# Writing down the order: the scheduler's order against the written one in the first layer's attention

## The chip, the cores and the metric

The kernel runs on one core of a Trainium2 chip. The core has TensorE (PE in the profile, its weight loads PEld), VectorE (DVE), ScalarE (ACT), GpSimd (POOL) and SyncE (SP), which here only issues DMAs. Each engine takes its instructions from a queue of its own, in order; they wait for each other by semaphores. The time is device microseconds of one execution, here the median of three runs.

## The reference

Four sequences of 512 tokens of width 128 go through two layers, all in f32. The first layer is a half-step of a "latent" block, a full attention and another half-step of the same latent block; the second layer mixes chosen tokens, runs four additive-attention blocks and mixes chosen tokens again.

```python
x = x + 0.5 * _L0_ffn_ref(_layernorm(x), ...)    # latent: causal attention, then mixture of experts
x = x + _L0_attn_ref(_layernorm(x), ...)         # full attention, 16 heads of 8
x = x + 0.5 * _L0_ffn_ref(_layernorm(x), ...)
x = x + 0.5 * _L1_ffn_ref(...)                   # chosen tokens
x = x + _L1_attn_ref(...)                        # four blocks
x = x + 0.5 * _L1_ffn_ref(...)
```

The change concerns the first three lines. `_L0_ffn_ref` normalizes x, runs a causal attention with 16 heads of 8, normalizes again, and sends each token to the best two of eight experts (hidden width 256, SiLU).

## The kernel before, in words

**Tasks and units.** `first_layer` makes twelve tasks: four causal ("latent") ones, one for each sequence, four full ones, four causal ones. They are numbered 0 to 11. A task is cut into units, each of which covers one 128x512 PSUM bank of scores for each of four row groups: 10 units in a causal task, 16 in a full one, 144 in all. Heads lie four to a row group; g counts the column groups of four heads.

**The loop.** `attention` walks once over all units, n = 0 to 151, and each step has two halves ("half-units"). In a step, three units are at work: unit n has its scores computed and their maxima taken (`maxima`, L527, PE; `reduce_max`, L543 for causal and L547 for full tasks, DVE); a unit five or six before has its scores computed again, transposed and with the maximum subtracted (`shifted`, L562, PE), then the exponential (`exponent`, L574, ACT) and, in causal tasks, the mask on the diagonal (`mask`, L580, POOL); a unit two steps before that is multiplied by the values (`products`, L605, PE).

When the last unit of a group g has its maxima, `place_maxima` transposes them (`mT`, L551, DVE) and four DMAs on SP (L555) write them into rows of `qA`, where L562 reads them as one more row of the contraction.

**What runs beside the units.** A half-unit also holds pieces of other work, written as generators that are stepped once per half-unit. `prepare` (L298 on) makes the next task's input during the present one: bn_stats of two chunks of X (L167); a half-unit later the other two and the aggregates `mv` (L171), then on POOL `v` (L312, in causal tasks also L316) and the root `r` (L154); a half-unit later four `h` (L323, POOL; task 0's on DVE); a half-unit later four `Y` (L336, POOL; in full tasks L328), then the transposes of `h` (L193, PE) and their copy (ACT). The projections (L267), their copies `qC` and `kC` and the DMAs that spread them over `qA` and `kA` (L363 to L366, SP) follow. A task's `prepare` begins with the first units of the task before it.

`gates` follows a causal task: the same kind of normalization with `h` in L686 on POOL, the gate's scores, a copy `lg` (L703), comparisons `more` and `same` on DVE (L709, L711) with two operations on POOL (L712, L718), `rank` (L725), `ex` (L727, ACT), `comb` (L731 to L737), and transposes of `comb` (L741, PE). Then `Mixture` adds, per half-unit, one expert half: L267 on PE, `th` (L467, ACT), `v` (L472, DVE), `hid` (L473, POOL), and three half-units later L267 again into `sum`.

**Banks.** `bank` picks one of eight PSUM banks by a small clock kept while the kernel is written out; the choice is made when the text is run and is the same whatever order the instructions get later.

**What sets the order.** The kernel's text is written out once as a list of instructions. A scheduler of the framework then puts each engine's instructions into an order of its own: it respects what they read and write and the buffers of the pools, and may otherwise move an instruction ahead of others that stand before it in the text. Two aids keep instructions where they are written: `tc.issue_after`, which is used once for the constants, and `tc.keep_in_program_order` for DMAs that load late weights. Here, `prepare`'s lines that the following speaks of:

```python
yield from moments_steps(X[:, b], mv)
...
r = rsqrt(v[:, 0:n], n)
yield
eng = nc.gpsimd if self.k else nc.vector
...
yield
```

Of the kernel before, what the change touches and what calls it, by code (L numbers as in the profile page):

```python
# [40 lines left out]
def tile_macaron(ctx: ExitStack, tc: tile.TileContext, a: dict, out: bass.AP):  # L41
    nc = tc.nc
# [68 lines left out]
    def constants_later():  # L111
        nc.gpsimd.tensor_copy(ident_h, ident)

        make_causal_mask(nc, paired, mask_val=NEG)
        nc.gpsimd.memset(paired[KSEL:P, 0:KSEL], NEG)

        nc.gpsimd.affine_select(
            out=before,
            in_=ones[:, 0 : NE * NE].rearrange("p (e f) -> p e f", f=NE),
            pattern=[[1, NE], [-1, NE]],  # L120
            compare_op=ALU.is_gt,
            fill=0.0,
            base=0,
            channel_multiplier=0,
        )

        nc.gpsimd.iota(
            slots, pattern=[[1, KSEL]], base=1, channel_multiplier=0, allow_small_or_imprecise_dtypes=True
        )
        nc.gpsimd.iota(  # L130
            places, pattern=[[1, T]], base=0, channel_multiplier=0, allow_small_or_imprecise_dtypes=True
        )

        nc.gpsimd.memset(mine, 0.0)
        for r in range(NPAIR):
            for i in range(2):
                nc.gpsimd.memset(mine[i * KSEL : (i + 1) * KSEL, r, 2 * r + i : 2 * r + i + 1], 1.0)

    def in_turn(runs):

        t = 0
        while runs:
            for start, run in list(runs):
                if start <= t and next(run, 0) == 0:
                    runs.remove((start, run))
            t += 1
# [85 lines left out]
    def first_layer(opened, picked):  # L232
        with (
# [18 lines left out]
            def heads_constants():  # L252
                constants()
                for i, vA in enumerate(vAs):

                    nc.gpsimd.memset(vA, 0.0)
                    split = vA.rearrange("p c (u s) k -> p (c u) s k", s=2)
                    for i in range(2):
                        nc.gpsimd.memset(split[:, :, i, 16 * i + HD : 16 * i + 2 * HD], 1.0)
                constants_later()  # L260
# [501 lines left out]
                heads_constants()  # L762
            tasks[0].spread()
            tasks[0].values()
            attention()
            streaming.close()
            top = opened()
            choosing = choice([0, 1], lambda b: (1, b) in mixed, top, picked)
# [524 lines left out]
    with ExitStack() as until_chosen:  # L1293

        def opened():
            return until_chosen.enter_context(tc.tile_pool(name="top", bufs=1, side="right"))

        chosen_first = first_layer(opened, {})
        made = tc.tile_pool(name="made", bufs=2)
        wp, ready = until_done.enter_context(made), {}  # L1300
        weights = additive_weights(wp, ready)
        chosen_attention(*chosen_first, beside=[(8, weights(0))])
# [73 lines left out]
```

## Time and profile before

| what | value |
|---|---|
| median of three runs | 1370.44 us (1369.15 to 1373.41) |
| span of the profiled execution | 1369.7 us |
| instructions in the profile | 29349 |
| PE busy | 1289.1 us (94%) |
| DVE busy | 954.4 us (70%) |
| ACT busy | 586.5 us (43%) |
| POOL busy | 562.1 us (41%) |
| mean granted TensorE clock | 0.968 |

For the profiled execution the profile gives its span and no other time; the span is 0.7 us below the median. The first layer's units take the span up to about 815 us. Times in the text are microseconds from the span's start. A line of the profile names the engine, the source line, the operation and the tiles, out<-in; "x4" counts merged instructions; what stands in brackets is the idle time of the engine before it and what ended it. A line of the list of waits has the engine and its instruction, who released it, then the total in us, how often, and the longest. A line of the table by stretches has, after the stretch and its length, the busy time and count of PE, PEld, DVE, ACT and POOL, the granted clock, the DMA share and GB/s. "PEld" idle times are not stalls where PE itself is busy.

### The profile page before, as it was taken

How to read it: one execution, taken by the hardware profiler on the slowest of the kernel's cores; microseconds unless marked ns; L12 is line 12 of the kernel's file. 1: busy time of each engine (PE TensorE's matmuls, PEld its weight loads, DVE VectorE, ACT ScalarE, POOL GpSimd, SP SyncE). 2: the span in 40 equal slices, each digit the busy share in tenths (PEclk: the TensorE clock that was granted, in tenths of full speed). 3: DMA queues.
4: the chain of work that ended last, by engine and by line, in shares of the span. 5: the costliest groups of instructions: out<-in, count | busy, mean ns of one | idle time of the engine just before them, and what ended most of it. 6: DMA issues, size and time to landing. Idle time of an engine off the chain costs nothing. (4 is left out here: it accounts for less than half of the span.)

```text
span 1369.7 us, 29349 instructions
## 1 busy us (share of the span) xinstructions
PE 1289.1 (94%) x11050; PEld 699.9 (51%) x11050; DVE 954.4 (70%) x3293; ACT 586.5 (43%) x1180; POOL 562.1 (41%) x823
## 2 busy tenths in 40 slices
PE   5998999999999999999999999989889999997897
PEld 2554445333333333465544443367667767665675
DVE  6886776666658777778767638687466776667773
ACT  1555454454556666665545443222223332323222
POOL 8345655544424112024564755622244443543100
PEclk8999999999999999999999999999979999999799
DMA  3001101020111100000111011211000100000000
GB/s 115 21 24 41 43 33 49 2 80 1 64 45 32 39 1 18 3 19 19 50 33 34 33 53 28 76 40 40 1 20 5 40 1 17 1 1 1 1 9 23
DMA packets 37172, 39.52 MB, mean 29 GB/s; under 512 B 11080, under 2 KB 23880, under 8 KB 37032
## 3 DMA queue, kind: packets, MB, share of 16 engines
q1 hardware_dynamic: 34536, 35.06, 8.3%
q10 hardware_dynamic: 2496, 2.59, 0.6%
q8 instruction: 87, 1.43, 0.4%
q14 instruction: 53, 0.43, 0.1%
HBM read 29.45 MB, written 1.18 MB: 22 GB/s over the span
## 5 line engine op out<-in xcount | busy, mean ns | idle before, releaser
L574 ACT ACTIVATE e<-bank 128x512 f32<-128x512 f32 x576 | 313.7, 595 | 278.4 <-PE bank L527 240.0
L527 PE MATMUL bank<-kA,qA 32*128 32x512 f32 (+3 forms) x1536 | 349.0, 527 | 4.1 <-DVE nm L543 1.8
L562 PE MATMUL bank<-qA,kA 32*128 32x512 f32 (+3 forms) x1536 | 334.0, 524 | 0.3 <-DVE nm L543 0.3
L543 DVE CUSTOM_DVE_ANT_0 junk<-bank,causal 128x384 f32<-128x384 f32 (+3 forms) x512 | 251.0, 490 | 89.5 <-PE bank L527 51.3
L547 DVE TENSOR_REDUCE nm<-bank 128x1 f32<-128x512 f32 x256 | 164.9, 686 | 78.9 <-PE bank L527 78.7
L473 POOL TENSOR_TENSOR hid<-v,spread 128x512 f32<-128x512 f32 x128 | 163.9, 1286 | 127.1 <-DVE v L472 101.7
L562 PEld LDWEIGHTS bank<-qA,kA 32*128 32x128 f32 x1536 | 129.5, 185 | 136.9 <-issue 54.1
L605 PE MATMUL sum<-e,vA 128*32 128x256 f32 (+1 forms) x2560 | 183.7, 368 | 6.1 <-POOL e L580 6.0
L580 POOL TENSOR_SCALAR_AFFINE_SELECT e<-e 128x256 f32<-128x256 f32 x256 | 99.3, 407 | 192.8 <-ACT e L574 191.7
L527 PEld LDWEIGHTS bank<-kA,qA 32*128 32x128 f32 x1536 | 147.4, 187 | 24.6 <-DVE nm L543 5.8
L605 PEld LDWEIGHTS sum<-e,vA 128*32 128x32 f32 x2560 | 62.8, 109 | 165.8 <-issue 134.0
L267 PE MATMUL sum<-hid,sb_f_w 128*32 128x512 f32 x1024 | 135.6, 597 | 3.0 <-POOL hid L473 2.9
L267 PE MATMUL bank<-tT,sb_f_w 128*32 128x512 f32 x1024 | 137.1, 602 | 0.0
L472 DVE SCALAR_TENSOR_TENSOR v<-th,bank 128x512 f32<-128x512 f32 x128 | 87.0, 681 | 43.9 <-ACT th L467 29.2
L467 ACT ACTIVATE th<-bank 128x512 f32<-128x512 f32 x128 | 76.3, 597 | 49.0 <-PE bank L267 39.5
L154 POOL TENSOR_TENSOR r<-v,mhalf 128x4 f32<-128x4 f32 (+1 forms) x64 | 71.8, 1123 | 5.1
L1250 PE MATMUL bank<-h2T,w 128*128 128x512 f32 x128 | 69.0, 632 | 0.2 <-ACT h2T L1239 0.2
L1256 PE MATMUL bank<-w,hid 128*128 128x128 f32 x512 | 65.7, 277 | 0.1
L1256 PEld LDWEIGHTS bank<-w,hid 128*128 128x128 f32 x512 | 63.1, 194 | 4.8 <-issue 1.5
L1251 ACT ACTIVATE hid<-bank,sb_l_cols 128x512 f32<-128x512 f32 x64 | 43.9, 688 | 39.9 <-PE bank L1250 39.8
L1148 PE MATMUL bank<-wa,hT 128*128 128x385 f32 x128 | 56.5, 540 | 1.4 <-ACT hT L1141 1.4
L312 POOL TENSOR_SCALAR v<-mv 128x4 f32<-128x4 f32 x12 | 2.8, 230 | 131.1 <-DVE mv L171 130.8
(279 smaller groups left out, 1805.4 us busy)
## 6 DMA issues: line engine op xcount, KB each, us to landing
spread<-away SPq DMA_DIRECT2D x64, 256.0 KB
qA<-mT SPq DMA_DIRECT2D x192, 2.0 KB
qA<-qC SPq DMA_DIRECT2D x11, 256.0 KB
kA<-kC SPq DMA_DIRECT2D x11, 256.0 KB
w<-in_l_w_dram SPq DMA_DIRECT2D x8, 256.0 KB
sb_m_wqkv<-in_m_wqkv_dram SPq DMA_DIRECT2D x4, 384.0 KB
m_yg<-in_m_trig_dram SPq DMA_DIRECT2D x8, 130.0 KB
X<-in_x_dram SPq DMA_DIRECT2D x4, 256.0 KB
```

What stands on the lines that cost most here:

```text
L267: nc.tensor.matmul(ps[32 * j : 32 * j + 32, :], lhsT=w[:, 32 * j : 32 * j + 32], rhs=rhs, start=start, stop=stop, skip_group_check=True,)
L467: nc.scalar.activation(th, ph, AF.Tanh, scale=0.5)
L472: nc.vector.scalar_tensor_tensor(v, th, 1.0, ph, ALU.add, ALU.mult)
L473: nc.gpsimd.tensor_tensor(hid, v, self.spread[e], op=ALU.mult)
L527: nc.tensor.matmul(ps[:, at : at + w], lhsT=t.qA[r0 : r0 + 32, g, c * P : (c + 1) * P], rhs=t.kA[r0 : r0 + 32, g, 0:w], start=True, stop=True,
L543: nc.vector.tensor_tensor_reduce(junk[:, 0:w], src, causal[:, T - w : T], 1.0, NEG, ALU.add, ALU.max, dst)
L547: nc.vector.tensor_reduce(dst, src, axis=AX.X, op=ALU.max)
L562: nc.tensor.matmul(ps[:, at : at + w], lhsT=t.kA[r0 : r0 + 32, g, kc * P : (kc + 1) * P], rhs=t.qA[r0 : r0 + 32, g, q0:T], start=True, sto ...
L574: nc.scalar.activation(es[n][:, j, :], ps, AF.Exp)
L580: nc.gpsimd.affine_select(out=e, in_=e, pattern=[[0, 2], [1, P]], compare_op=ALU.is_ge, fill=0.0, base=0, channel_multiplier=-1,)
L605: nc.tensor.matmul(to[32 * j : 32 * j + 32, q0 + lo - at : q0 + hi - at], lhsT=t.vA[:, kc, 4 * j + g, :], rhs=es[n][:, j, lo:hi], start=fresh,
L1256: nc.tensor.matmul(pm[:, c * P : (c + 1) * P], lhsT=hid[:, f, c * P : (c + 1) * P], rhs=w2[:, f, :], start=(f == 0), stop=(f == 3),)
```

## The change

After `attention()` has written its instructions, a new function `pinned` goes through those instructions and ties each one on DVE, POOL, PE and ACT to the one before it on the same engine, by a dependency without a semaphore. The scheduler thereby loses its choice on these four engines for the units' stretch; SP is not in the set. What comes before `attention()` (the first task's `prepare`, the constants) and behind it (the rest of the mixture, the second layer) is left to the scheduler as before.

```diff
+    def pinned(engines, since):
+
+        last = {}
+        for i in list(nc.cur_bb.bb.instructions)[since:]:
+            if i.engine in engines:
+                if i.engine in last:
+                    tc.add_manual_dep(
+                        i,
+                        last[i.engine],
+                        mybir.DependencyInfo(mybir.DependencyClass.NoSync, mybir.DependencyReason.DATA),
+                        reason="program order",
+                    )
+                last[i.engine] = i.name
+
     def in_turn(runs):
...
             tasks[0].spread()
             tasks[0].values()
+            since = len(nc.cur_bb.bb.instructions)
             attention()
+            pinned({mybir.EngineType.DVE, mybir.EngineType.Pool, mybir.EngineType.PE, mybir.EngineType.Activation}, since)
             streaming.close()
```

In the two built programs each engine has the same instructions. PE's order is the same. On DVE, 2621 instructions, task 2's last aggregate goes from place 32 to 104, that of task 8 from 634 to 742. On POOL, 823 instructions, task 2's first `h` goes from place 59 to 79. The transposes `mT` (L551) stand up to eight reductions later.

## The prediction

> **What bounds the kernel now.** I read the sums by stage first, then TensorE's waits, then the timeline around each stall. By stage (columns: stretch, its length, then busy us of PE, PEld, DVE, ACT, POOL with counts, granted clock, DMA share, GB/s):
>
> ```profile
> 21.00:64.00 43.00, 38.28 (x336) 20.76 (x336) 34.94 (x143) 17.62 (x33) 24.45 (x47) 0.88 0.06 18
> 90.00:116.00 26.00, 21.47 (x215) 11.75 (x216) 17.76 (x78) 11.71 (x23) 18.85 (x34) 0.87 0.01 2
> 250.00:270.00 20.00, 18.80 (x164) 8.49 (x162) 10.98 (x24) 7.96 (x15) 6.84 (x13) 0.83 0.01 2
> 400.00:557.00 157.00, 157.00 (x1444) 55.89 (x1440) 116.53 (x218) 97.88 (x183) 31.40 (x41) 1.00 0.08 23
> 640.00:665.00 25.00, 21.98 (x210) 12.62 (x209) 18.09 (x73) 11.85 (x23) 18.22 (x32) 0.93 0.01 1
> ```
>
> The attention of the first layer runs to about 815 us, and TensorE is busy in nearly all of it (157.00 of 157.00 us in the fourth row). What it waits for is therefore added to the end. The waits of PE up to 815 us (us in total, times, longest):
>
> ```profile
> PE sum L605 <- POOL e L580: 6.0, 2, 3.7
> PE bank L193 <- POOL h L323: 4.4, 4, 3.5
> ```
>
> The first is two stalls, at 106.7 and 648.2 us. The second is almost wholly one: task 1's transposes wait 3.45 us for `h` at 26.47 (three more waits of 0.30 follow it). At the transposes of tasks 2 to 11 PE waits 0.27 us at most. Why, task 8 shows: its `h` is made 80 us ahead (GpSimd, then PE):
>
> ```profile
> 420.52 1.67 POOL L154 TENSOR_TENSOR r<-v,mhalf 128x8 f32<-128x8 f32 x1
> 422.29 3.13 POOL L323 TENSOR_SCALAR h<-X,mv,r 128x128 f32<-128x128 f32 x4
> ...
> 505.16 0.66 PE L193 MATMUL bank<-ident,h 128*128 128x128 f32 x4
> ```
>
> **The change, part by part.** Instructions, shapes and counts stay. In the built program PE's order is the same in both kernels, ScalarE moves seven small `ex` (L727) and one copy, and SyncE's queue shifts by five places at most. What moves is VectorE and GpSimd, above all `prepare`: `mv` of task 2 goes from place 32 on VectorE to 104, of tasks 7 to 10 from 625, 634, 714, 795 to 661, 742, 825, 900. PE still reaches the transposes at its old place, so each task's chain must now fit in the two half-units that the text leaves it.
>
> *The chain of one `prepare`.* Behind the last reduction of its half-unit: two bn_stats and four bn_aggr 0.8 us (0.87 for four stats and 0.36 for the aggregates at 412.78); handover 0.1; `v` 0.57 for two (420-422 us: L312, L316, then `r`) or 0.3 for one; `r` 1.67 (128x8, causal tasks) or 1.04 (128x4, full tasks); handover 0.1; four `h` 3.13; the last transpose 0.3. That is 6.7 us causal, 5.8 full. Masks (0.4 each, L580) or `hid` (1.27, L473) that now stand between on GpSimd come on top. From the reduction's end in the profile to the transposes' end there were:
>
> - task 2: reduction 61.60, +6.7, two masks 0.8: 69.1 for 64.80, +4.3
> - task 3: 105.64, +6.7 +0.8: 113.1 for 115.55 (a time that holds the stall at 106.7): -2.4
> - task 4: 200.58, +5.8 +0.4 +1.3: 208.1 for 206.00, +2.1
> - task 5: 273.64, +5.8 +0.4: 279.8 for 278.12, +1.7
> - task 6: `hid` ends 361.57, +3.4: 365.0 for 364.01, +1.0
> - task 7: 441.65, +5.8: 447.4 for 444.99, +2.4
> - task 8: 502.48, +6.7: 509.2 for 505.82, +3.4
> - task 9: 564.00, +6.7: 570.7 for 566.66, +4.0
> - task 10: 604.35, +6.7 +0.4: 611.4 for 607.48, +3.9
> - task 11: behind a gate's `h` chain on GpSimd; 645.00 +0.8, `v` 0.9, `r` 1.5, two masks 0.8, `h` 2.4, then mask, `v`, `r`, mask, `h`, transpose 6.5: 658 for 655.53, +2.5
>
> Sum 22.9, I take **23**. Behind each stalled transpose stand on PE the next half-unit's scores, so VectorE and ScalarE starve too. Bounds 13 to 26: below, where VectorE is the pace (it has no idle time over 0.3 us from 36 to 64) it still holds about 2 us of scores and part of the stall is covered; above, the list with one more mask each.
>
> *The start.* Task 1's `mv` (done at 12.8 before) now stands behind two units of reductions, which end at 26.01. With 1.2 of stats, `v` 0.5, `r` 1.67, `h` begins at 29.7 for 25.62, so PE's 3.45 us wait grows by about 4. Unit 3 shifts by 4, and its eight reductions now stand ahead of the first `mT` (L551, 30.11 before): 39.5, its four DMAs until 41.7 and some 1.6 to land (packets of the last end at about 33.9 for an issue at 32.29). The first L562 starts at about 43.3 for 36.51. VectorE works on in that time, so it loses 5 and PE 7. I take **6**, bounds 4 and 9. The later 47 `mT` come 1 to 5 us later and keep 1 us or more between landing and the L562 that reads them (tightest at 85 and 458 us); they cost nothing, and about 1 us a task if that cover is gone (inside the upper bound). On SyncE the `qC`, `kC` and `spread` transfers now stand ahead of `mT` transfers in some places, 0.4 to 0.6 us of issue each: the same cover hides them.
>
> *The gates.* `comb` (L731 to L737, 1.4 us) and `rank` now follow 10 to 13 us later. Against the transposes L741 that read them this leaves 0.9, 0.7 and 1.1 us short (125.88, 192.94, 672.08) and nothing elsewhere: **+2**, bounds 0 and 3. `h` of the gates (L686) had 6 to 9 us to spare mostly and comes 4 to 5 later: nothing.
>
> *What goes away.* GpSimd no longer runs `h` and `Y` in one block ahead of the masks, nor VectorE `rank` right behind `more`:
>
> ```profile
> 106.33 3.27 POOL L336 TENSOR_SCALAR Y<-X,mv,r 128x128 f32<-128x128 f32 x4
> 109.56 1.49 POOL L580 TENSOR_SCALAR_AFFINE_SELECT e<-e 128x256 f32<-128x256 f32 x4
> ...
> 110.39 1.08 PE L605 MATMUL sum<-e,vA 128*32 128x256 f32 x8 [3.72 <-POOL e L580]
> ...
> 261.37 1.65 PE L527 MATMUL bank<-kA,qA 32*128 32x512 f32 x2 [1.20 <-ACT e L574]
> ```
>
> The stalls at 106.7 and 648.2 are already in tasks 3 and 11 above. The one at 260.2 (VectorE's `comb` chain between two reductions) is worth 1.2 and up to 3.4 of slow clock; two of 0.62 and 0.85 at 662 and 728 follow a wait of `rank` for `more`. **-5**, bounds -8 and -3.
>
> *The clock.* After 3.72 us of waiting the granted clock is 0.5 for 6.83 us, after 2.33 us for 3.41, after 1.20 us (at 261.8) for 6.83; after 0.85 not at all. A stretch of 3.41 costs 1.7 while PE is the bound. Tasks 2, 8, 9, 10 would open with waits of 2.3, 1.4, 2.1, 2.0 us, followed by three of 0.3 to 0.5 between transposes. I take 3.5 such stretches: **+6**, bounds 0 (none) and 17 (five at 3.4).
>
> The Trainium skill speaks against this term: TensorE: Matmul & The Clock Gate, section "HAM oscillation — how this bites in real kernels", has it that idle gaps above about 3.4 us bring the slow clock. By it only the start's second wait would count, the term would be 0 to 3 and the sum some 4 us lower; the gaps of 1.20 and 2.33 us here differ from it, and I go by them.
>
> **The sum.** 23 + 6 + 2 - 5 + 6 = 32 us on 1370.4. The profiled execution's span is 1369.7, 0.7 below the median of the three runs, so I add to the median: **1402**. Bounds together: 13 + 4 + 0 - 8 + 0 = 9 and 26 + 9 + 3 - 3 + 17 = 52: 1379 to 1422 for this case alone.
>
> **The rivals.**
>
> *Faster: the blocks on GpSimd were the dearer evil.* The stalls that the scheduler's order makes are 3.7 + 2.4 (slow clock) at 106.7, 2.3 + 1.7 at 648, 4.6 at 260 and 1.5: 16 us. If the transposes cost nothing, 1354. For it: GpSimd's masks stand free of blocks. Against: the chain of 6.7 us stands between a reduction and transposes that follow it by 2.7 to 3.3 us in tasks 2 and 8 to 10. It decides if PE arrives there more than 3.5 us later, relative to VectorE, than in this profile.
>
> *No change.* PE's order is identical and the moves might all lie in idle time: within 4 us of 1370. Against: the slack of 82 and 68 us at tasks 8 and 10 is gone by the order alone.
>
> *Much slower.* The stalls add up with slow clock at each of ten transposes (10 x 3.4) and a start of 9: 23 + 9 + 3 + 34 - 3 = 66, so 1436. For it: 10.24 us of half clock followed the one such wait there is. Against: that wait was 3.45 us in one piece; most new ones are below 2.4.
>
> **How the numbers follow.** Slower inside 1379 to 1422: 0.75. Much slower: 0.10. Faster: 0.11. No change: 0.04. The range takes the bounds, with 2 us below for what 0.3% of measurement may add, and reaches up to 1428 for half of the much slower case: 1377 to 1428 holds 0.80. Slower by over 0.3% (about what three runs that lie within 0.3% can tell from no change) has 0.75 + 0.10, faster 0.11, same 0.04.
>
> **What the changed profile would show.** PE L193 waits for POOL `h` L323 some 15 to 25 us in total over about ten tasks, where it was 4.4; the first L562 at about 43 us; PE's wait for POOL `e` L580 and VectorE's for `more` nearly gone; more short stretches at clock 0.5 between 60 and 660 us; all after 815 as it was, only shifted. I am wrong if L193's waits stay below 8 us (then the chain is shorter, or PE later, than I read it), or if the waits are there and the time is not (then VectorE's or GpSimd's backlog, not PE, sets the pace).

## The result, and the profile after

The changed kernel takes 1401.94 us (median of four runs, 1400.40 to 1402.07), the kernel before 1369.80 in the same comparison (1367.79 to 1373.41): the ratio is 1.0225, with a 95% interval of 1.0207 to 1.0242. The forecast was 1402. In the two profiled executions the spans are 1369.7 and 1398.6 us, 28.9 apart; the medians are 32.1 apart. What follows accounts for the 28.9, since rows exist only for these. One time in the runs below, 6653.82 us, stands far outside the nine others of its kernel (TensorE and ScalarE bound) and is not in its ratio. Line numbers of the changed kernel are 14 higher up to the units' end (L193 is now L207, L323 is L337).

Three rows of TensorE's waits up to 850 us in the changed kernel (us in total, times, longest):

```profile
PE bank L207 <- POOL h L337: 32.8, 39, 7.5
PE bank L755 <- DVE comb L751: 2.5, 4, 0.9
PE bank L576 <- DMA qA<-mT: 1.5, 1, 1.5
```

The first row was 4.4 us with 4 waits. The row of waits for `e`, 6.0 us before, is gone, and so is VectorE's wait of `rank` for `more`, which was this in the kernel before:

```profile
DVE rank L725 <- POOL more L718: 10.4, 7, 5.6
```

The sums by stage of the changed kernel, for the stretches that the prediction showed and two more (stretch, length, busy us of PE, PEld, DVE, ACT, POOL with counts, granted clock, DMA share, GB/s):

```profile
21.00:64.00 43.00, 33.04 (x256) 17.96 (x256) 31.17 (x135) 13.70 (x25) 14.75 (x29) 0.80 0.04 14
90.00:116.00 26.00, 25.49 (x289) 14.16 (x286) 21.93 (x88) 14.94 (x29) 10.84 (x26) 1.00 0.09 27
250.00:270.00 20.00, 20.00 (x205) 8.08 (x199) 13.25 (x30) 8.63 (x16) 13.46 (x21) 1.00 0.01 2
400.00:557.00 157.00, 152.88 (x1372) 53.73 (x1364) 105.54 (x189) 91.21 (x171) 17.84 (x21) 0.98 0.09 26
510.00:525.00 15.00, 12.56 (x88) 3.97 (x84) 7.24 (x18) 6.50 (x12) 8.36 (x11) 0.77 0.01 2
557.00:640.00 83.00, 75.98 (x741) 37.35 (x744) 57.23 (x208) 43.69 (x81) 24.50 (x42) 0.94 0.03 9
640.00:665.00 25.00, 24.77 (x296) 14.40 (x288) 21.02 (x88) 15.31 (x29) 8.32 (x22) 1.00 0.08 25
```

TensorE now comes 11 us later at 106, 13 at 260 and 28 at 648, so rows of the same times hold different work, and the full rows from 90, 250 and 640 on don't show by themselves that the stalls of before are gone. The instructions that had waited there show it: L605 at 110.39 (a wait of 3.72 us) now starts at 117.98, L527 at 261.37 (1.20) at 272.64 and L605 at 650.54 (2.33) at 675.65, all without a wait:

```profile
117.98 0.64 PE L619 MATMUL sum<-e,vA 128*32 128x256 f32 x8
...
675.65 0.64 PE L619 MATMUL sum<-e,vA 128*32 128x256 f32 x8
```

The loss stands elsewhere: TensorE loses 5 us of its 38 at the start, 4 us between 400 and 557 where it had lost none, and 7 us between 557 and 640, where the kernel before had this row:

```profile
557.00:640.00 83.00, 82.67 (x910) 47.16 (x911) 67.25 (x270) 50.11 (x93) 16.86 (x44) 1.00 0.05 16
```

The row 510 to 525 holds task 8's transposes. This is the timeline there (start, duration, engine, line, operation; in brackets the idle time before and its releaser):

```profile
513.13 0.36 DVE L185 BATCH_NORM_AGGREGATE mv<-st 128x2 f32<-128x6 f32 x4
513.58 0.23 POOL L326 TENSOR_SCALAR v<-mv 128x4 f32<-128x4 f32 x1 [57.30 <-DVE mv L185]
514.17 1.67 POOL L168 TENSOR_TENSOR r<-v,mhalf 128x8 f32<-128x8 f32 x1
515.94 3.14 POOL L337 TENSOR_SCALAR h<-X,mv,r 128x128 f32<-128x128 f32 x4
516.80 0.33 PE L207 MATMUL bank<-ident,h 128*128 128x128 f32 x1 [1.23 <-POOL h L337]
517.58 0.33 PE L207 MATMUL bank<-ident,h 128*128 128x128 f32 x1 [0.45 <-POOL h L337]
518.36 0.47 PE L207 MATMUL bank<-ident,h 128*128 128x128 f32 x1 [0.45 <-POOL h L337]
```

GpSimd, which had made this `h` 80 us ahead, has now been idle for 57.30 us when `mv` comes. The chain from `mv` to the end of the fourth `h` is 5.95 us long (513.13 to 519.08), and TensorE stands at its end: it takes each piece of `h` 0.1 us after it is made, waits 1.23, 0.45, 0.45 and 0.30 us, and the half clock begins at 518.2 and lasts 6.83 us.

The same instruction of TensorE can be looked up in both traces, since its order is the same. Its start after minus its start before, read on both sides of each event, gives the account:

| event | shift, us | change |
|---|---|---|
| start, to 60 | 0 to 5.83 | +5.83 |
| task 2's transposes | 5.83 to 11.38 | +5.55 |
| the stall before at 106.7 not there, then task 3 | 11.38 to 6.2 to 10.08 | -1.30 |
| task 4 | 8.25 to 13.07 | +4.82 |
| the stall before at 260 not there, nor its slow clock | 13.07 to 7.54 | -5.53 |
| tasks 5, 6, 7 | 7.54 to 10.34 | +2.80 |
| task 8 | 10.34 to 16.39 | +6.05 |
| task 9 | 16.39 to 22.98 | +6.59 |
| task 10 | 22.98 to 28.46 | +5.48 |
| the stall before at 648 not there, then task 11 | 28.46 to 25.0 to 32.1 | +3.64 |
| 660 to 672 (`rank` no longer waits, then `comb` is late) | 32.1 to 29.86 to 30.97 | -1.13 |
| 728 (`rank` no longer waits) | 30.51 to 28.55 | -1.96 |
| drift in between (-2.29), and from 728 to the end (+0.61) | | -1.68 |
| sum | | 29.16 |

Behind the units the shift stays between 27.5 and 29.8 us: little has changed there.

### The profile page after: what moved, and what is told of

It is laid out like the page before. It is cut to its first block, busy times and chain, and to the rows that moved or that the text cites. A ratio compares the mean times of both kernels' runs of the same rounds, so it can differ in the third digit from the quotient of the medians.

```text
span 1398.6 us, 29350 instructions
## 1 busy us (share of the span) xinstructions
PE 1293.7 (92%) x11050; PEld 701.5 (50%) x11050; DVE 952.2 (68%) x3293; ACT 586.1 (42%) x1180; POOL 563.2 (40%) x823
## 5 line engine op out<-in xcount | busy, mean ns | idle before, releaser
L576 PE MATMUL bank<-qA,kA 32*128 32x512 f32 (+3 forms) x1536 | 337.3, 533 | 1.5 <-DMA qA<-mT 1.5
L576 PEld LDWEIGHTS bank<-qA,kA 32*128 32x128 f32 x1536 | 130.9, 188 | 139.3 <-issue 51.9
L207 PE MATMUL bank<-ident,h 128*128 128x128 f32 x144 | 38.8, 331 | 46.2 <-POOL h L337 32.8
L1267 ACT ACTIVATE hid<-bank,sb_l_cols 128x512 f32<-128x512 f32 x64 | 44.0, 689 | 37.8 <-PE bank L1266 37.5
```

The lines of the kernel that those rows point to most:

```text
L576: nc.tensor.matmul(ps[:, at : at + w], lhsT=t.kA[r0 : r0 + 32, g, kc * P : (kc + 1) * P], rhs=t.qA[r0 : r0 + 32, g, q0:T], start=True, sto ...
```

## The experiments

The theory, **A**: the loss is the late chain of `prepare`, from the statistics through `v`, `r` and `h` to the transposes. **A1** has it that the place of the statistics on VectorE makes it late, **A2** the place of `h` behind masks on GpSimd. The rival, **B**: the loss is spread over the gates, `mT` and the mixture, and `prepare` is a small part.

### Which engine's order

Only VectorE's order, or only GpSimd's, or only TensorE's and ScalarE's is bound; the rest is left to the scheduler. The three versions each have one of the added lines. Times of different comparisons may be set side by side here: the kernel before had medians of 1368.8 to 1369.8 us in them.

```diff
-            pinned({mybir.EngineType.DVE, mybir.EngineType.Pool, mybir.EngineType.PE, mybir.EngineType.Activation}, since)
+            pinned({mybir.EngineType.DVE}, since)
+            pinned({mybir.EngineType.Pool}, since)
+            pinned({mybir.EngineType.PE, mybir.EngineType.Activation}, since)
```

VectorE alone:

> Only VectorE keeps the written order; GpSimd, ScalarE and TensorE are left to the scheduler. Theory A1 (the loss comes from the bn_stats and aggregates that stand behind the reductions, and the transposes of h then wait for the whole chain): the waits of PE L193 for h stay at 20 to 33 us and the time is 1392 to 1404. Theory A2 (the loss comes from GpSimd, where h now stands behind masks and hid): the waits fall below 12 us and the time is under 1382. Theory B (the loss is spread over gates, mT and the mixture's operations on VectorE, prepare is a small part): the time is over 1390 but the waits for h are below 15 us.

Measured: 1392.65 us, ratio 1.0175 (1.0159 to 1.0190); TensorE waits 27.5 us for `h` in 35 waits. Both are as A1 had it, the time at the lower end of its range.

GpSimd alone:

> Only GpSimd keeps the written order; VectorE is left to the scheduler, which makes the statistics early. Theory A1: mv and r are there in time, so only h itself (3.1 us) can be late, behind the masks of its half-unit: 0 to 2.5 us at each of six tasks, against 6 to 11 us for the blocks on GpSimd that go away; 1360 to 1376. Theory A2: 1390 to 1402, with waits of PE for h over 20 us. Theory B: within 4 us of the kernel before, no wait for h that grows.

Measured: 1393.62 us, ratio 1.0178 (1.0147 to 1.0208). This missed A1's 1360 to 1376. The time lies in A2's range, but A2's sign does not hold: TensorE waits 15.4 us for `h`, not over 20, which leaves much of the loss without a row of TensorE's. VectorE's waits name more of it, and the timeline near 114 us one case (GpSimd alone bound):

```profile
DVE rank L739 <- POOL more L732: 22.0, 7, 5.1
```

```profile
113.60 3.12 POOL L337 TENSOR_SCALAR h<-X,mv,r 128x128 f32<-128x128 f32 x4
...
117.50 0.72 POOL L732 TENSOR_TENSOR more<-more,same 128x256 f32<-128x256 f32 x1
118.25 0.42 DVE L739 TENSOR_REDUCE rank<-more 128x32 f32<-128x256 f32 x1 [5.08 <-POOL more L732]
```

The scheduler puts `rank` early on VectorE; bound to the text, GpSimd makes four `h` first and `more` only behind them, at 117.50, and the reductions behind `rank` stand. Two orders that each fit themselves don't fit each other. Whether this is the whole miss is asked below.

TensorE and ScalarE:

> Only TensorE and ScalarE bound to the written order; VectorE and GpSimd by the scheduler as before. All theories: TensorE's order is the same by either way and ScalarE moves seven ex and a copy, so 1366 to 1374, no wait for h above 5 us, and the stalls for e at about 107 and 648 us remain. If it is outside 1364 to 1376, ScalarE's order is a term that the sum lacks.

Measured: 1367.79 us, ratio 0.9982 (0.9965 to 0.9999). No wait for `h` above 3.5 us, and the two stalls for `e` remain (6.5 us). By themselves, these two engines' order costs nothing.

### Prepare alone against all the rest

All four engines are bound, but the instructions that `prepare` issues on VectorE and GpSimd are left out of the binding, so that the scheduler places them.

```diff
+    loose = set()
+
+    def unbound(run):
+        while True:
+            at = len(nc.cur_bb.bb.instructions)
+            more = next(run, 0) != 0
+            for i in list(nc.cur_bb.bb.instructions)[at:]:
+                if i.engine in (mybir.EngineType.DVE, mybir.EngineType.Pool):
+                    loose.add(i.name)
+            if not more:
+                return
+            yield
...
-            if i.engine in engines:
+            if i.engine in engines and i.name not in loose:
...
-                        background.append(t.prepare())
+                        background.append(unbound(t.prepare()))
```

> Written order on all four engines, except for the VectorE and GpSimd instructions of prepare (statistics, v, r, h, Y), which the scheduler may place. Theory A (the chain of prepare is the loss): the waits of PE for h fall to 4 to 6 us; what stays is the first mT behind unit 3 (3 us) and comb (2.5 us), what stays away are some of the 5 to 11 us of stalls behind blocks on GpSimd; 1364 to 1378. Theory B: 1388 or more.

Measured: 1368.75 us, ratio 0.9995 (0.9983 to 1.0008). With `prepare` free on VectorE and GpSimd the loss is gone as a whole; B is out. That it is no faster than before although VectorE's `rank` and the masks are in the written order has a row (this kernel's waits of TensorE):

```profile
PE bank L221 <- POOL h L714: 9.3, 2, 5.0
PE bank L221 <- POOL h L351: 3.6, 4, 2.7
```

`h` of the gates (L714) now stands behind `prepare`'s block of `r` and `Y` on GpSimd, and TensorE waits for it 4.24 us at 107 and 5.01 at 648: the stalls of before, with another tile waited for.

Then the two engines apart: only GpSimd's part of `prepare` free (the condition in `unbound` is `i.engine == mybir.EngineType.Pool`), and only VectorE's part (`mybir.EngineType.DVE`).

> The changed kernel, but the GpSimd instructions of prepare (v, r, h) are not bound to the written order; VectorE's stats of prepare are. Theory C (one chain: whichever link is late makes the transposes late): h can't begin before the stats, which stay at their late places, so most of the loss stays: 1383 to 1397, with 12 to 28 us of waiting for h on TensorE. Theory A2 (only h's place behind GpSimd's masks costs): 1364 to 1378, with under 10 us of waiting for h.

Measured: 1393.00 us, ratio 1.0171 (1.0151 to 1.0192).

> The changed kernel, but the VectorE instructions of prepare (its stats) are not bound to the written order; GpSimd's v, r and h of prepare are. Theory C (one chain: whichever link is late makes the transposes late): with the stats early, what is left is h behind the masks of its half-unit, 10 to 20 us of waiting on TensorE, and no wait of rank for more on VectorE: 1376 to 1390. Theory A1 (only the place of the stats costs): 1364 to 1376, with under 8 us of waiting for h. Theory A2 (only h's place costs): 1392 to 1402.

Measured: 1378.28 us, ratio 1.0065 (1.0040 to 1.0090). TensorE's waits for `h`, in the first kernel and in the second:

```profile
PE bank L221 <- POOL h L351: 27.9, 35, 7.5
```

```profile
PE bank L221 <- POOL h L351: 15.6, 26, 1.9
```

With the statistics late, freeing `h` recovers 8.9 of 33.2 us; with the statistics early and `h` still in the written order, 23.7. Against the version with both free (1368.75) the late statistics cost 24.3 and the place of `h` 9.5, together 33.8, where the whole change costs 33.2 against that version. The two links add up; the ranges of theory C (whichever link is late makes the transposes late) held, and A1 is the larger part of it, not all.

### What made GpSimd's order alone dear

VectorE and GpSimd are bound as in the last version, but the VectorE instructions of the gates are free too, so `rank` goes back to its early place.

```diff
-                        beside.append(gates(self))
+                        beside.append(unbound(gates(self)))
```

> The version with only the stats of prepare free on VectorE (1378.3), and the VectorE instructions of the gates free as well; GpSimd stays bound. Theory R (GpSimd's order alone cost 24 us because the scheduler puts the gates' rank on VectorE where the written order of GpSimd makes more only later): VectorE's wait of rank for more comes back to 18 to 24 us, and the time is 1388 to 1396. Rival (it was the scheduler's order of the reductions and of the hidden layer on VectorE that doesn't fit GpSimd's written order): rank waits for more under 5 us or its waits don't count, and the time stays at 1376 to 1381.

Measured: 1386.49 us, ratio 1.0128 (1.0104 to 1.0151), just below theory R's range. VectorE's wait of `rank` for `more` is back at 21.8 us, and TensorE's waits for `h` are 15.8 as without it. So the gates' instructions on VectorE account for 8.2 of the 15.3 us between 1378.28 and 1393.62. The other 7.1 lie in what that run leaves to the scheduler besides, the rest of VectorE's work and the order on TensorE and ScalarE; no run tells which of it, and the size is rough, since the interval of 1393.62 is 4 us wide to either side.

### Room for the chain

The text is given three more half-units between `h` and its transposes, from task 1 on (`Y` comes later with the transposes); everything stays bound.

```diff
                         )
                     yield
+                    if self.k:
+                        yield
+                        yield
+                        yield
                     if self.part == "full":
```

> As the changed kernel, but in the text the transposes of h come three half-units later (three more empty steps of prepare for tasks 1 to 11), so that the chain of 6 to 7 us has five half-units instead of two. Nothing else moves. Theory A: all waits for h go, with the slow clock behind them; of the start only the wait for the first mT stays (3 us); the stalls behind masks at 106 and 648 us and that at 260 us stay away: 1356 to 1368, faster than the kernel before. Theory B: over 1388. A rival inside A (the slow clock comes from elsewhere and stays): 1366 to 1376 with half clock of over 40 us up to 815 us.

Measured: 1361.44 us, ratio 0.9945 (0.9929 to 0.9962), 40.5 us below the changed kernel and faster than the kernel before. The waits for the `h` of tasks 1 to 11 are gone from TensorE's list up to 850 us, and the stretches of tasks 8 to 10 are full at clock 1.00:

```profile
400.00:557.00 157.00, 157.00 (x1452) 56.81 (x1448) 113.57 (x211) 97.67 (x182) 14.00 (x19) 1.00 0.07 21
557.00:640.00 83.00, 82.48 (x898) 46.68 (x892) 66.41 (x278) 47.91 (x89) 34.30 (x68) 1.00 0.05 16
```

The same three half-units in the kernel before, without any binding:

> The kernel before (order by the scheduler) with the same three extra half-units between h and its transposes that gained 40 us in the written order. Theory A (the scheduler makes h far ahead anyway, so there is no stall there to take away; the gain needs the written order, whose stalls it removes): the time stays within 4 us of before, 1365 to 1373, and the stalls at about 107 and 648 us for e remain. Rival (the three half-units are worth something whatever the order, by a later place of the transposes): 1356 to 1363.

Measured: 1376.91 us, ratio 1.0067 (1.0044 to 1.0091). Both expectations missed: it is 8 us slower. The stalls for `e` are still there (7.1 us), and at the two lines of scores TensorE waits 5.8 us for the maxima `nm`, where it was 2.3 before. Why the scheduler's order gets worse by it was not followed up. What it settles is that the gain of the three half-units needs the written order.

### The start

The binding begins with unit 6, so that the scheduler orders what is issued before.

```diff
+                    if n == 6:
+                        marked.append(len(nc.cur_bb.bb.instructions))
...
-            pinned({mybir.EngineType.DVE, mybir.EngineType.Pool, mybir.EngineType.PE, mybir.EngineType.Activation}, since)
+            pinned({mybir.EngineType.DVE, mybir.EngineType.Pool, mybir.EngineType.PE, mybir.EngineType.Activation}, marked[0])
```

> The changed kernel, but bound to the written order only from unit 6 on, so that the scheduler orders what is issued before. Theory A (the start is a term of 6 us of the loss): task 1's transposes wait about 3.5 us for h instead of 7.5, the first scores-times-values product starts near 36.5 us instead of 43.2, and the time is 1394 to 1398. Rival (VectorE works on through the start's stall, so nothing but the idle time on TensorE moves): the same first signs, but 1400 to 1403, with the shift of TensorE's instructions at 66 us the same 11 us as in the changed kernel.

Measured: 1394.34 us, ratio 1.0179 (1.0155 to 1.0203): 7.6 us less than the changed kernel. Task 1's transposes wait 1.45 us and then three times 0.3, the first L576 starts at 35.63, and TensorE's shift is 4.4 us at 66 and 6.2 behind task 2, where it was 11.1 and 11.4. The rival, that VectorE works on through the stall, is out.

### All together

Three half-units, the binding from unit 6 on, and one `yield` more ahead of the transposes of `comb`.

> The changed kernel with three edits: the three extra half-units between h and its transposes (from the second task on), the order as written bound only from unit 6 on so that the scheduler orders the start, and one more half-unit between comb and the transposes of comb in the gates. Theory A (each stall on TensorE was a term of its own): against the version with the three half-units alone, 1361.4, the start gives back 3 to 6 us and the waits for comb 1.7 us, so 1353 to 1358; TensorE's waits up to 815 us then hold at most 4.5 us for h (task 1 alone) and under 1 us for comb, and the half-clock stretch of 20 us near the start becomes about 10. Rival (the start is not worth anything by itself, since VectorE is the pace there and works on): 1360 to 1362, with the first scores-times-values product earlier but the second unit's end where it was.

Measured: 1357.05 us, ratio 0.9907 (0.9888 to 0.9925). No wait for `h` of `prepare` is left on GpSimd's side, and none for `comb`. It is the fastest version here, 12 us below before and 45 below the changed kernel. One sign missed: the stretch of half clock at the start did not shrink to 10 us; it is 20.48 us as with the three half-units alone (see the end).

## Why the prediction was right

The time came out as forecast, by the cause that was named. By its steps:

- **The chains of `prepare`, 23, and the clock, 6.** The row of waits is 32.8 us; without task 1's 8.4 that leaves 24.4 at the ten later tasks (the sign of 15 to 25 us in total fits these, not the whole row). But the 23 of the list had the stalls at 106.7 and 648 (3.72 and 2.33 us) already taken off in tasks 3 and 11; what it is to be set beside is at most 18.4, so it was 5 us or more too high. The waits at the transposes are 3.6, 2.8 and 3.2 us for tasks 2 to 4, 2.7 for 5 to 7 together (listed: 5.1), 2.4, 3.5, 3.3 and 2.9 for 8 to 11. In the account above, where the clock is in, these tasks make +33.6, after the stalls of 106.7 and 648 are taken off, against 29 for both terms. What the waits leave over fits the clock: tasks 2 to 11 have 37.5 us of half clock, the two stalls before had 10.2, and the 27.3 more cost up to 13.7 us where 6 was taken (inside the bound of 17). The mis-sized step is "3.5 such stretches" of 3.41: seven of tasks 2 to 11 have one, three of them of 6.83 or 10.24.
- **The start, 6.** 5.8 in the account, 7.6 by the run that leaves the start to the scheduler. Task 1's wait is 7.46 us (3.45 plus 4.0) and the first L576 starts at 43.17, as worked out.
- **The gates, +2.** The waits for `comb` are 2.5 us; the shift moves by 1.1 at the one at 672.
- **What goes away, -5.** -5.5 at 260, -2.2 at 665, -2.0 at 728: -9.7, outside the lower bound of -8. Another 1.7 us went in a drift that the sum doesn't have. So the losses and the gains were both sized too small, and the errors nearly cancel; the right total is partly luck.
- **The page against the clock term.** The Trainium skill, TensorE: Matmul & The Clock Gate, section "HAM oscillation — how this bites in real kernels", sets about 3.4 us as the gap from which the slow clock comes. Waits of 1.23 (task 8), 1.47 (task 3) and 1.82 us (task 4), each followed by up to three of 0.45, were followed here by 6.83, 3.41 and 3.41 us at clock 0.5. By the page's rule the term would have been 0 to 3 us, as the prediction estimated; the measurement decides against it in this kernel.
- **The rivals.** "Faster" had its gain right: the stalls that the scheduler's order makes are gone. It failed on its condition, since TensorE comes too early for the chain: at seven of the ten later tasks it waits 1.2 to 2.3 us for the first piece of `h`. The versions with room for the chain show what it would take: they collect that gain, 1361 and 1357 us for the 1354 that the rival gave. In the first of them TensorE's shift falls by 4.3 us at 106, 5.3 at 260, 4.6 from 648 to 665 and 2.0 at 728, together the rival's 16. "Much slower" took the half clock of 10.24 us at the start to follow task 1's wait of 3.45 us; in that trace the clock falls at 22.90 us and the wait begins at 23.02, so the wait did not bring it, and in the three versions without that wait the stretch is longer still, 20.48 us (see the end).

## What to carry to other kernels

Where a text order is to take a scheduler's place, look for what the scheduler had moved far ahead: a chain over two engines (here 6 us from the aggregates to the last `h`) needs as much distance in the text as it takes, and three more half-units turned a loss of 2.25% into a gain of 0.55%. An order bound on one engine has to fit the orders of the engines it exchanges work with: GpSimd's written order beside a VectorE that the scheduler had ordered brought 22.0 us of waiting for `more`, and cost 15 us more than with VectorE bound too but for the statistics. Binding all four was no remedy by itself, since it was the slowest of all (1401.94). Each wait of 1 to 2 us on a busy TensorE is to be priced with the slow clock that may follow, by estimate 1.7 to 5.1 us more here (half of the 3.41 to 10.24 us that followed).

## What the runs showed of the hardware

Up to 850 us the granted clock in the traces falls in pieces of 3.41 us or multiples of it, and is 0.5 in them. The length of a wait does not settle whether it falls: a single wait of 1.20 us at 261 in the kernel before was followed by 6.83 us of half clock, one of 1.22 us at 808 in the fastest version by none. Nor does the clock need waits to stay down: in the kernel before with three more half-units, TensorE works without a wait from 21.06 us on, after waits of 1.09 and 0.56 us, and yet the clock is 0.5 for 20.48 us from 22.5 on. The sums of that kernel from 21 to 64 us, and its timeline:

```profile
21.00:64.00 43.00, 42.60 (x297) 21.07 (x301) 33.02 (x134) 15.41 (x29) 23.64 (x45) 0.76 0.04 15
```

```profile
19.69 0.81 PE L531 MATMUL bank<-kA,qA 32*128 32x256 f32 x3
21.06 11.27 PE L531 MATMUL bank<-kA,qA 32*128 32x256 f32 x36 [0.56 <-DVE nm L547]
32.26 1.11 PE L193 MATMUL bank<-ident,h 128*128 128x128 f32 x4
```

TensorE is busy in 42.60 of 43.00 us at a mean clock of 0.76. The two fastest versions have the same stretch of 20.48 us there; at half clock it costs up to 10 us, which none of these runs won back. What brings it is open.
